# A two-layer transformer on one core: another order for the tail, and two sums moved from GpSimd to VectorE

## The chip, the cores and the metric

The kernel runs on one core of one Trainium2 chip. The core has five engines that work in parallel and wait for each other by semaphores: TensorE (PE in the profile; PEld are its weight loads), VectorE (DVE), ScalarE (ACT), GpSimd (POOL) and SyncE (SP), which here only issues transfers. Each engine takes its instructions strictly in the order of its own list. The metric is the device time of one execution in microseconds, and lower is better. All data is float32.

## The reference

Two transformer layers over 8 batches of 256 tokens with 128 channels. In each layer the normalised and modulated input goes through causal attention, and then through a mixture of experts of which every token uses two. Cut to what matters here, the second layer's expert part is:

```
def _L1_ffn_ref(x, gate_w, gate_b, shared_wg, shared_wu, shared_wd, experts_wg, experts_wu, experts_wd):
    router_logits = sigmoid(x @ gate_w + gate_b)
    expert_values, expert_indices = top_k(router_logits, k=2)
    expert_values = expert_values / sum(expert_values)
    hg = einsum('bsd,edi->bsei', x, experts_wg)          # 16 experts, 64 hidden channels
    hu = einsum('bsd,edi->bsei', x, experts_wu)
    all_outputs = einsum('bsei,eid->bsed', silu(hg) * hu, experts_wd)
    selected = take_along_axis(all_outputs, expert_indices[..., None], axis=2)
    expert_weighted = sum(expert_values[..., None] * selected, axis=2)
    return x + _mlp(x, shared_wg, shared_wu, shared_wd) + expert_weighted

x = x + ga * _L1_attn_ref(layernorm(x) * (1 + ca) + sa, ...)
h = layernorm(x) * (1 + cb) + sb
x = x + gb * _L1_ffn_ref(h, ...)
```

`ga`, `ca`, `sa` and `gb`, `cb`, `sb` are rows of a modulation, one for each batch.

## The kernel before

The 2048 tokens are kept in four wide tiles `x[0]` to `x[3]`, 512 tokens (two batches) each, as 128 partitions by four groups of 128 channels. `TT` is 4, the groups of a wide tile, and `LAST` is 3, the last wide tile. From line 1058 on nothing is reordered by a scheduler: the order of the calls is, engine by engine, the order of the instructions. The loops over layer 0 and over the attention of layer 1 come first. The tail, lines 2016 to 2126, is a list of calls written out by hand; it begins when the last attention scores are done.

In the tail the second layer's experts are computed in two ways.

For the first three wide tiles the tokens have been sorted by expert into a table `xs` in HBM. It is read in 40 small tiles of 128 rows, four at a time, as ten "quads" m = 0 to 9:

- `fetch_rows1(m)` (line 1738) has SyncE load four small tiles. `turn1(m)` (1775) transposes them on TensorE, copies the result to `xT` on ScalarE, and then calls `fetch_rows1(m + 4)`.
- `fetch_weights1(m)` (1753) is for the quads 4 to 9, whose experts are known only at run time: SyncE reads four row numbers and issues four loads of 128 KB into `wt`.
- `hidden1(m)` (1785): eight pairs of matmuls into a PSUM buffer of tag "s" (there are two), Silu on ScalarE, product on VectorE into `aq`.
- `project_tiles(m)` (1798): four matmuls, two copies on VectorE into `ysb` (three buffers), and SyncE stores the 256 KB to the table `ys` in HBM.
- When all of `ys` is written, `gather1(j)` (1900), for j = 0 to 11, has GpSimd issue two indirect transfers each, which bring every token's two expert results into `yg`.
- `combine1(j)` (1906): ScalarE multiplies one result with its weight into `tc` (two buffers), VectorE adds the other times its weight. After each fourth, `tc` is multiplied with the modulation `gb`, added to `x[w]`, and SyncE stores `x[w]` to the output. These two steps are done by GpSimd for w = 0 and 1, and by VectorE for w = 2.

For the last wide tile the experts are computed densely, with eight pairs p = 0 to 7 of experts:

- `dense_hidden(p)` (1849): four matmuls of 512 columns into a buffer of tag "s", Silu on ScalarE, product on VectorE into `a` (the function `gated`, 1842).
- `gate_rows(k)` (1823) transposes the gates of one batch, and SyncE spreads them through HBM over the partitions into `gp`, which `dense_gate(p)` (1855) multiplies with `a` on VectorE.
- `dense_project(p)` (1859): eight matmuls that add to `outs[LAST]` in PSUM.

The shared expert runs over two wide tiles at once: `shared_hidden(w)` (1867) and `shared_project(w)` (1878) for w = 0 and 2. `ffn1_add(w)` (1891) multiplies a wide tile of `outs` with `gb` on VectorE and adds it to `x[w]`.

Between them lie the ends of attention and routing of the last two batches: `spread_last` (1642) and `finish1` (1654) end the attention of batch 7. `norms[0]` and `norms[1]` are lists of five steps for batches 6 and 7 (`norm1`, 1675: measure, normalise with a square root on ScalarE, modulate into `h`, and two steps of GpSimd that make `ht` and add it to `x`). `go6` and `go7` are the steps of `route1` (1699) for these batches, one for each call: logits on TensorE and Exp on ScalarE; first half of the top-2 search on VectorE; second half; weights and gates. `judge` and `flag` (1920) check on VectorE that all softmax sums were in range; the last instruction of the tail writes `bad`, which every engine then loads before a branch around a slower path that is not taken.

ScalarE holds one set of functions at a time: a change between Silu, Exp and square root brings an instruction ACT_TABLE_LOAD.

Of the kernel before, what the change touches and what calls it, by code (L numbers as in the profile page):

```python
# [17 lines left out]
B, S = 8, 256  # L18
# [539 lines left out]
def fast_path(ctx: ExitStack, tc: tile.TileContext, i: dict, out: bass.AP, bad: bass.AP):  # L558
# [224 lines left out]
    def of_batches(rows, w):  # L783

        return rows[:, bass.ts(w, 2), :].unsqueeze(2).to_broadcast([P, 2, 2, P])

    def by_batch(t):
        return t.rearrange("p (b j) c -> p b j c", j=2)
# [807 lines left out]
    def values1(b, u):  # L1596
        v = st1["v", b, u // 2]
        if u == 0:
            st1["s", b] = pp.tile([P, S], F32, tag="sum", bufs=1, name=f"sum1_{b}")
            st1["ou", b] = lp.tile([P, 2, 4, S], F32, tag="ou", name=f"ou1_{b}")  # L1600
        s = st1["s", b]
        o = pp.tile([P, 2, S], F32, tag="o", bufs=1, name=f"o1_{b}_{u}")
        pts = [st1.pop(("pt", b, 2 * u + m)) for m in range(2)]
        for m in range(2):
            for kb, cols, qs in blocks:
                for n in range(2):
                    nc.tensor.matmul(  # L1607
                        out=o[bass.ts(n, D1), m, qs], lhsT=v[:, kb, bass.ts(4 * (u % 2) + 2 * m + n, D1)],
                        rhs=pts[m][:, n, cols], start=(kb == 0), stop=(kb == 1), skip_group_check=True,
                    )  # L1610

        for kb, cols, qs in blocks:
            for m in range(2):
                for n in range(2):
                    nc.tensor.matmul(
                        out=s[bass.ts(2 * n + m, 32), qs], lhsT=on[:, u, :], rhs=pts[m][:, n, cols],
                        start=(kb == 0 and u == 0), stop=(kb == 1 and u == 3), skip_group_check=True,
                    )
        nc.vector.tensor_copy(st1["ou", b][:, :, u, :], o)

    def reciprocals1(b):
        r = st1["r", b] = lp.tile([P, S], F32, tag="r", name=f"r1_{b}")
        nc.vector.reciprocal(r, st1.pop(("s", b)))
        if b == B - 1:
            return

        rd = dp1.tile([2, NC1, S], F32, tag="rd", name=f"rd1_{b}")
        nc.sync.dma_start(out=rd.rearrange("n c q -> (n c) q"), in_=r[0:P:8, :])
        rb = lp.tile([P, 2, 4, S], F32, tag="rb", bufs=1, name=f"rb1_{b}")
        for n in range(2):  # L1630
            nc.sync.dma_start(
                out=rb[bass.ts(n, D1)].rearrange("p m u q -> p (m u q)"),
                in_=rd[n].rearrange("c q -> (c q)").partition_broadcast(D1),
            )
        st1["rb", b] = rb
        judge(r)
# [116 lines left out]
    def fetch_weights1(m):  # L1753

        tag, n = {4: ("wt", 2), 5: ("wt", 2), 9: ("rb", 1)}.get(m, ("v", 3))
        wt = sq["w", m] = lp.tile([P, 4, WD1], F32, tag=tag, bufs=n, name=f"wt1_{m}")
        for t in range(4):
            d = 4 * m + t - E1
            if t == 0:
                _, rs = nc.values_load_multi_w_load_instructions(  # L1760
                    z1.widx[0:1, d : d + 4], engines=[mybir.EngineType.SP], min_val=0, max_val=(E1 - 1) * P,
                    skip_runtime_bounds_check_because="an expert's number, 128 times",
                )
            nc.sync.dma_start(out=wt[:, t, :], in_=i["wpk1"][bass.ds(rs[t], P), :])
# [10 lines left out]
    def turn1(m):  # L1775
        xT_ps = ps_ln([P, 4, P], f"xT1_{m}")
        xg = sq.pop(("x", m))
        for t in range(4):
            nc.tensor.transpose(xT_ps[:, t, :], xg[:, t, :], ident)
        xT = sq["xT", m] = lp.tile([P, 4, P], F32, tag="xT", name=f"xTs1_{m}")  # L1780
        nc.scalar.copy(xT, xT_ps)
        if m + 4 < NQ:
            fetch_rows1(m + 4)

    def hidden1(m):
        xT = sq.pop(("xT", m))
        gu = pp.tile([P, 2, 2, P], F32, tag="s", name=f"gu1_{m}")
        for what in range(2):
            for t in range(4):
                nc.tensor.matmul(  # L1790
                    out=gu[bass.ts(t % 2, I1), what, t // 2, :], lhsT=weights1(m, t)[what],
                    rhs=xT[:, t, :], start=True, stop=True,
                )
        a = sq["a", m] = lp.tile([P, 2, P], F32, tag="aq", name=f"aq1_{m}")
        nc.scalar.activation(a, gu[:, 0], AF.Silu)
        nc.vector.tensor_tensor(a, a, gu[:, 1], ALU.mult)

    def project_tiles(m):
        a = sq.pop(("a", m))
        y = [pp.tile([P, 2, P], F32, tag=tag, bufs=1, name=f"yq1_{m}_{tag}") for tag in ("o", "sum")]  # L1800
        for t in range(4):
            k = t % 2
            nc.tensor.matmul(
                out=y[k][:, t // 2, :], lhsT=a[bass.ts(k, I1), t // 2, :], rhs=weights1(m, t)[2],
                start=True, stop=True,
            )
        ysb = lp.tile([P, 2, 2, P], F32, tag="ysb", bufs=3, name=f"ysb1_{m}")
        for k in range(2):
            nc.vector.tensor_copy(ysb[:, :, k, :], y[k])
        nc.sync.dma_start(  # L1810
            out=z1.ys[bass.ds(4 * m * P, 4 * P), :].rearrange("(t p) c -> p t c", p=P),
            in_=ysb.rearrange("p a k c -> p (a k) c"),
        )
# [92 lines left out]
    def combine1(j):  # L1906
        w, n = divmod(j, TT)
        if n == 0:
            sums[w] = lp.tile([P, TT, P], F32, tag="ht", name=f"tc1_{w}")
        t = sums[w]  # L1910
        yg, g = sums["yg", j // 3][:, j % 3], g12_1[:, j, :]
        nc.scalar.activation(t[:, n, :], yg[:, 0, :], AF.Copy, scale=g[:, 0:1])  # L1912
        nc.vector.scalar_tensor_tensor(t[:, n, :], yg[:, 1, :], g[:, 1:2], t[:, n, :], ALU.mult, ALU.add)  # L1913
        if n == TT - 1:
            eng = nc.gpsimd if w < 2 else nc.vector
            eng.tensor_tensor(by_batch(t), by_batch(t), of_batches(mdb1[:, GB], w), ALU.mult)  # L1916
            eng.tensor_tensor(x[w], x[w], t, ALU.add)  # L1917
            nc.sync.dma_start(out=out[:, bass.ts(w, TT), :], in_=x[w])

    def flag():  # L1920
# [95 lines left out]
    norms = [norm1((b, 1)) for b in (B - 2, B - 1)]  # L2016
    go6, go7 = (one(route1((b, 1))) for b in (B - 2, B - 1))
    values1(*divmod(N - 1, 4))
    reciprocals1(B - 1)
    turn1(0)  # L2020
    hidden1(0)
    turn1(1)
    turn1(2)
    hidden1(1)
    add()
    project_tiles(0)
    fetch_weights1(7)
    turn1(3)
    project_tiles(1)
    fetch_weights1(8)  # L2030
    fetch_weights1(9)
    hidden1(2)
    turn1(4)
    tables()
    hidden1(3)
    norms[0][0]()
    project_tiles(2)
    turn1(5)
    norms[0][1]()
    hidden1(4)  # L2040
    project_tiles(3)
    turn1(6)
    hidden1(5)
    norms[0][2]()
    project_tiles(4)
    turn1(7)
    hidden1(6)
    hidden1(7)
    norms[0][3]()
    project_tiles(5)  # L2050
    go6()
    turn1(8)
    norms[0][4]()
    project_tiles(6)
    turn1(9)
    go6()
    hidden1(8)
    project_tiles(7)
    hidden1(9)
    go6()  # L2060
    project_tiles(8)
    spread_last()
    project_tiles(9)
    for j in range(TT * LAST): gather1(j)
    shared_hidden(0)
    go6()
    finish1(B - 1)
    norms[1][0]()
    gate_rows(0)
    norms[1][1]()  # L2070
    norms[1][2]()
    norms[1][3]()
    shared_project(0)
    go7()
    shared_hidden(2)
    go7()
    dense_hidden(0)
    go7()
    dense_hidden(1)
    go7()  # L2080
    shared_project(2)
    ffn1_add(0)
    dense_hidden(2)
    dense_hidden(3)
    gate_rows(1)
    ffn1_add(1)
    ffn1_add(2)
    dense_hidden(4)
    dense_hidden(5)
    judge(st1["r", B - 1])  # L2090
    norms[1][4]()
    judged = flag()
    next(judged)
    dense_hidden(6)
    dense_gate(0)
    dense_gate(1)
    dense_hidden(7)
    combine1(0)
    dense_gate(2)
    dense_project(0)  # L2100
    combine1(1)
    dense_project(1)
    dense_gate(3)
    dense_project(2)
    dense_project(3)
    combine1(2)
    combine1(3)
    dense_gate(4)
    combine1(4)
    dense_gate(5)  # L2110
    dense_gate(6)
    dense_project(4)
    combine1(5)
    combine1(6)
    combine1(7)
    dense_gate(7)
    dense_project(5)
    combine1(8)
    combine1(9)
    dense_project(6)  # L2120
    dense_project(7)
    combine1(10)
    combine1(11)
    ffn1_add(LAST)
    next(judged, None)
    nc.sync.dma_start(out=out[:, bass.ts(LAST, TT), :], in_=x[LAST])
    manual.close()
    l1.close()

# [93 lines left out]
```

## Time and profile before

| | us |
| --- | --- |
| median of six runs | 642.28 |
| lowest and highest of them | 638.04, 644.18 |
| the profiled execution, measured as a run | 643.22 |
| its span, first to last instruction | 641.4 |

Busy time over the whole span: TensorE 544.3 us (85%), VectorE 347.4 (54%), GpSimd 300.7 (47%), ScalarE 274.3 (43%). The chain that ended last, followed back from the last instruction, is short and lies in the tail. These are its pieces from 619.32 us on, with the start, the length and what ran:

```profile
619.32 0.62 DVE tc L1913 x2
619.94 0.07 issue
620.01 1.66 POOL tc L1916
621.67 0.07 issue
621.74 1.81 POOL x L1917
623.54 0.02 issue
623.56 0.70 ACT tc L1912 x2
...
625.47 3.15 DVE tc L1913 x4
628.62 0.02 issue
628.64 0.70 DVE tc L1916
629.34 0.02 issue
629.37 0.69 DVE x L1917
630.06 0.61 DVE tf L1894
630.67 0.02 issue
630.69 0.69 DVE x L1895
631.38 0.12 DVE bad L1927
```

A row of a timeline, as shown further on, reads: start in us from the span's first instruction, duration, engine (SPq are SyncE's issues), line, operation, what it writes `<-` what it reads, shape, how many in a row; in brackets the engine's idle time before it and what ended that. "Remote" there means that no instruction was found beside the semaphore's change, and "issue" that the profile shows nothing the engine waited for. Ends of matmuls are modelled, their starts are recorded.

### The profile page before, as it was taken

To read this page: it belongs to the slowest core of one execution; us is meant where nothing else is said; L and a number is where in the kernel's file an instruction comes from. 1 tells how busy PE (TensorE), PEld (TensorE's weight loads), DVE (VectorE), ACT (ScalarE), POOL (GpSimd) and SP (SyncE) were. 2 spreads that over 40 slices of the span, in tenths; PEclk is the share of its full clock that TensorE was granted. 3 is DMA by queue.
4 is the path that set the end of the run, shared out by engine and by line. 5 is a ranking of instruction groups with operands and counts; after the bars stand their busy time and mean duration, and the time that the engine had idled before them with its cause. 6 is when DMAs were issued, how large, how long until landed. Compare 5 with 4: busy or idle time off the path is not lost. (4 is left out here: it accounts for less than half of the span.)

```text
span 641.4 us, 11930 instructions
## 1 busy us (share of the span) xinstructions
PE 544.3 (85%) x4391; PEld 384.1 (60%) x4391; DVE 347.4 (54%) x1069; ACT 274.3 (43%) x486; POOL 300.7 (47%) x456
## 2 busy tenths in 40 slices
PE   3798879788699999699999999999999988883580
PEld 3444434455699897566676767666777666650250
DVE  3348897865532221356436664666565766541393
ACT  1485666544155554166334532445353424321130
POOL 7356697866124441465611447513646441047421
PEclk9999988879799999799999999999999998797796
DMA  8999970120349994220302031303030356524031
GB/s 280 344 408 401 388 279 14 55 98 26 108 141 328 308 317 152 108 74 26 88 5 67 9 80 34 80 1 67 21 81 18 72 160 182 166 72 106 20 84 55
DMA packets 52911, 85.41 MB, mean 133 GB/s; under 512 B 6428, under 2 KB 32156, under 8 KB 51692
## 3 DMA queue, kind: packets, MB, share of 16 engines
q1 hardware_dynamic: 44444, 59.77, 29.2%
q0 software_dynamic: 8400, 24.78, 12.2%
q8 instruction: 37, 0.61, 0.4%
q14 instruction: 30, 0.25, 0.1%
HBM read 53.46 MB, written 31.07 MB: 132 GB/s over the span
## 5 line engine op out<-in xcount | busy, mean ns | idle before, releaser
L812 POOL TENSOR_SCALAR_AFFINE_SELECT pt<-pt 128x256 f32<-128x256 f32 (+1 forms) x176 | 88.7, 530 | 108.3 <-ACT pt L1588 79.4
L1047 POOL DMA_INDIRECT yg<-ys,yidx x56 | 53.5, 956 | 52.2 <-DMA ys<-ysb 33.9
L1588 ACT ACTIVATE pt<-sc 128x768 f32<-128x768 f32 x64 | 48.4, 808 | 26.4 <-PE sc L1585 26.3
L1039 POOL DMA_INDIRECT wt<-in_wpk_dram,widx x31 | 29.2, 942 | 51.7 <-PE xT L1329 49.2
L1141 ACT ACTIVATE pt<-sc 128x1024 f32<-128x1024 f32 x48 | 46.5, 1023 | 15.6 <-PE sc L1137 12.4
L1340 ACT ACTIVATE hst<-hp,wt 128x128 f32<-128x128 f32 x136 | 38.9, 368 | 31.5 <-ACT hst L1340 18.8
L1585 PEld LDWEIGHTS sc<-q,k 64*128 64x128 f32 x512 | 41.5, 187 | 16.5 <-issue 11.5
L1585 PE MATMUL sc<-q,k 64*128 64x256 f32 (+1 forms) x512 | 50.5, 336 | 0.0
L1607 PE MATMUL o<-pt,v 128*64 128x256 f32 (+1 forms) x512 | 48.7, 332 | 1.8 <-POOL pt L812 1.8
L1570 ACT COPY v<-vp 128x512 f32<-128x512 f32 x32 | 18.8, 586 | 67.7 <-PE vp L1567 59.6
L1350 DVE COPY ysb<-yt 128x128 f32<-128x128 f32 x39 | 11.4, 292 | 60.4 <-PE yt L1346 60.4
L1607 PEld LDWEIGHTS o<-pt,v 128*64 128x64 f32 x512 | 31.9, 136 | 19.7 <-POOL pt L812 5.6
L1558 DVE COPY q<-qp 128x512 f32<-128x512 f32 x32 | 22.0, 689 | 39.3 <-PE qp L1554 37.7
L1137 PE MATMUL sc<-qm,k 32*128 32x512 f32 x192 | 36.9, 701 | 4.6 <-ACT pt L1141 3.8
L1338 PE MATMUL hp<-xTs,wt 128*128 128x128 f32 x272 | 36.5, 277 | 4.3 <-DMA wt<-in_wpk_dram,widx 3.3
L1554 PE MATMUL qp<-h,wq 128*128 128x256 f32 x128 | 37.1, 413 | 1.3 <-DVE sh L1299 1.3
L924 POOL DMA_INDIRECT xs<-ht0b,idx x32 | 31.7, 990 | 13.5 <-issue 4.6
L1567 PE MATMUL vp<-wv,h 128*128 128x512 f32 x64 | 35.9, 643 | 1.2 <-DVE q L1558 1.2
L1338 PEld LDWEIGHTS hp<-xTs,wt 128*128 128x128 f32 x272 | 33.0, 192 | 5.9 <-issue 2.5
L1346 PE MATMUL yt<-wt,hst 128*128 128x128 f32 x272 | 35.8, 275 | 0.0
L1558 ACT COPY k<-kp 128x512 f32<-128x512 f32 x32 | 18.8, 588 | 35.6 <-PE kp L1554 34.6
L1554 PE MATMUL kp<-h,wk 128*128 128x256 f32 x128 | 33.6, 386 | 0.0
(296 smaller groups left out, 1131.8 us busy)
## 6 DMA issues: line engine op xcount, KB each, us to landing
xs<-zero SPq DMA_DIRECT2D x1, 12288.0 KB
xs<-zero SPq DMA_DIRECT2D x1, 8192.0 KB
rb<-rd SPq DMA_DIRECT2D x14, 512.0 KB
mdb<-mrd SPq DMA_DIRECT2D x2, 2048.0 KB
xg<-xs SPq DMA_DIRECT2D x63, 64.0 KB
wt<-in_wpk_dram SPq DMA_DIRECT2D x24, 128.0 KB
wst<-in_wpk_dram SPq DMA_DIRECT2D x5, 514.0 KB
ys<-ysb SPq DMA_DIRECT2D x10, 256.0 KB
```

The lines of the kernel that those rows point to most:

```text
L812: nc.gpsimd.affine_select(out=pt, in_=pt, compare_op=ALU.is_ge, fill=0.0, base=0, pattern=[[0, pt.shape[1]], [1, P]], channel_multiplier=-1,)
L1047: nc.gpsimd.indirect_dma_start(out=yg[:, k, :], out_offset=None, in_=self.ys[:, :], in_offset=bass.IndirectOffsetOnAxis(ap=self.yidx[:, j, ...
L1137: nc.tensor.matmul(out=sc[:, n, :].rearrange("p (a q) -> p a q", q=rhs.shape[2]), lhsT=k[r, cols], rhs=rhs, start=True, stop=True,)
L1141: nc.scalar.activation(pt[:, bass.ts(half, 2), :], sc, AF.Exp)
L1338: nc.tensor.matmul(out=hp[:, c, :], lhsT=wt[:, bass.ts(c, P)], rhs=xT, start=True, stop=True)
L1340: nc.scalar.activation(hs[:, c, :], hp[:, c, :], AF.Gelu_apprx_tanh, bias=wt[:, WB + c : WB + c + 1])
L1554: nc.tensor.matmul(out=ps_[:, n, :], lhsT=w1[f"w{what}1"][:, bass.ts(2 * u + n, P)], rhs=hb, start=True, stop=True)
L1558: copy(st1[what, b, u], ps_)
L1567: nc.tensor.matmul(out=vp, lhsT=hb[:, bass.ts(j, P)], rhs=w1["wv1"][:, bass.ts(half, 512)], start=True, stop=True)
L1585: nc.tensor.matmul(out=sc[:, n, cols], lhsT=k[r, m, bass.ts(kb, P)], rhs=q[r, m, qs], start=True, stop=True)
L1588: nc.scalar.activation(pt, sc[:, :, 0:384], AF.Exp, scale=1.0 / math.sqrt(D1))
L1607: nc.tensor.matmul(out=o[bass.ts(n, D1), m, qs], lhsT=v[:, kb, bass.ts(4 * (u % 2) + 2 * m + n, D1)], rhs=pts[m][:, n, cols], start=(kb == ...
```

## The change

Two things. In `combine1` the multiplication with `gb` and the sum into `x[w]` are on VectorE for all three wide tiles; GpSimd has none of them any more. And the calls of the tail stand in another order. No call is added or left out, and none changes what it computes.

```
         if n == TT - 1:
-            eng = nc.gpsimd if w < 2 else nc.vector
-            eng.tensor_tensor(by_batch(t), by_batch(t), of_batches(mdb1[:, GB], w), ALU.mult)
-            eng.tensor_tensor(x[w], x[w], t, ALU.add)
+            nc.vector.tensor_tensor(by_batch(t), by_batch(t), of_batches(mdb1[:, GB], w), ALU.mult)
+            nc.vector.tensor_tensor(x[w], x[w], t, ALU.add)
             nc.sync.dma_start(out=out[:, bass.ts(w, TT), :], in_=x[w])
```

The order of the calls, before and after, stage by stage (several calls to a line; `g6` is `go6()`, `n0.2` is `norms[0][2]()`, `hid`, `proj`, `turn` are `hidden1`, `project_tiles`, `turn1`):

```
before:
 turn0 hid0 turn1 turn2 hid1 add proj0 fetch_weights1(7) turn3 proj1 fetch_weights1(8) fetch_weights1(9)
 hid2 turn4 tables hid3 n0.0 proj2 turn5 n0.1 hid4 proj3 turn6 hid5 n0.2 proj4 turn7 hid6 hid7 n0.3
 proj5 g6 turn8 n0.4 proj6 turn9 g6 hid8 proj7 hid9 g6 proj8 spread_last proj9
 gather1 x12  shared_hidden(0) g6 finish1(7) n1.0 gate_rows(0) n1.1 n1.2 n1.3
 shared_project(0) g7 shared_hidden(2) g7 dense_hidden(0) g7 dense_hidden(1) g7 shared_project(2)
 ffn1_add(0) dense_hidden(2) dense_hidden(3) gate_rows(1) ffn1_add(1) ffn1_add(2)
 dense_hidden(4) dense_hidden(5) judge n1.4 flag (minimum) dense_hidden(6) dense_gate(0) dense_gate(1)
 dense_hidden(7) combine1(0) dense_gate(2) dense_project(0) combine1(1) dense_project(1) dense_gate(3)
 dense_project(2) dense_project(3) combine1(2) combine1(3) dense_gate(4) combine1(4) dense_gate(5)
 dense_gate(6) dense_project(4) combine1(5..7) dense_gate(7) dense_project(5) combine1(8) combine1(9)
 dense_project(6) dense_project(7) combine1(10) combine1(11) ffn1_add(3) flag (bad) store x[3]
after:
 turn0 turn1 hid0 hid1 turn2 add proj0 fetch_weights1(7) turn3 proj1 fetch_weights1(8)
 hid2 turn4 tables hid3 n0.0 proj2 hid4 turn5 n0.1 turn6 proj3 n0.2 proj4 hid5 g6 turn7
 proj5 hid6 hid7 fetch_weights1(9) n0.3 g6 n0.4 turn8 proj6 hid8 turn9 proj7 g6 hid9 proj8 spread_last proj9
 finish1(7) g6 n1.0  gather1 x12  shared_hidden(0) gate_rows(0) n1.1 n1.2 shared_hidden(2) n1.3
 g7 g7 shared_project(0) shared_project(2) g7 dense_hidden(0) ffn1_add(0) dense_hidden(1) g7
 dense_hidden(2) n1.4 ffn1_add(1) dense_hidden(3) gate_rows(1) dense_hidden(4) dense_hidden(5) ffn1_add(2)
 judge dense_gate(0) dense_gate(1) dense_hidden(6) dense_hidden(7) dense_project(0) dense_gate(2)
 dense_gate(3) dense_project(1) dense_project(2) combine1(0) dense_project(3) combine1(1) combine1(2)
 dense_gate(4) combine1(3) dense_gate(5) combine1(4) dense_gate(6) dense_gate(7) combine1(5..7)
 flag (minimum) dense_project(4) combine1(8) dense_project(5) dense_project(6) combine1(9) combine1(10)
 dense_project(7) combine1(11) ffn1_add(3) store x[3] flag (bad)
```

## The prediction

> **What bounds the kernel now.** I read the times first, then the chain that ended last, then each engine's timeline from 515 us on. Before 525.7 us the two programs hold the same instructions; from there to the end the order differs. Four stages follow one another in this tail.
>
> *Stage 1, 526 to 568 us: SyncE's queue.* The timeline of SyncE's issues (start, us, what) and two of VectorE's rows:
>
> ```profile
> 541.90 4.69 SPq L1764 DMA_DIRECT2D wt<-in_wpk_dram  x8
> 546.84 1.88 SPq L1035 DMA_DIRECT2D xg<-xs  x4
> 548.82 0.38 SPq L1810 DMA_DIRECT2D ys<-ysb  x1
> 549.45 1.92 SPq L1035 DMA_DIRECT2D xg<-xs  x4
> 551.47 14.21 SPq L1810 DMA_DIRECT2D ys<-ysb  x7
> ```
>
> ```profile
> 551.30 0.42 DVE L1809 COPY ysb<-yq_o 128x256 f32<-128x256 f32 x1 [2.14 <-DMA ys<-ysb]
> 553.95 0.43 DVE L1809 COPY ysb<-yq_o 128x256 f32<-128x256 f32 x1 [1.79 <-DMA ys<-ysb]
> ```
>
> SyncE issues one transfer about every half microsecond without a pause: eight weight loads (quads 8 and 9), then the rows of quad 8, a result store, the rows of quad 9, and so on. The stores are late, so VectorE waits 2.14 and 1.79 us for a free `ysb` buffer, and TensorE stands behind it. The stage ends when the tenth store lands.
>
> *Stage 2, 568 to 601 us: the gathers.*
>
> ```profile
> 568.55 1.01 POOL L1047 DMA_INDIRECT yg<-ys,yidx  x1 [22.39 <-DMA ys<-ysb]
> 569.86 0.96 POOL L1047 DMA_INDIRECT yg<-ys,yidx  x1 [0.31 <-issue]
> ...
> 597.41 0.95 POOL L1047 DMA_INDIRECT yg<-ys,yidx  x1 [0.30 <-issue]
> 598.38 0.73 POOL L1683 TENSOR_TENSOR ht<-xn1b,mdb 128x256 f32<-128x256 f32 x1
> ```
>
> ```profile
> 590.02 0.60 ACT L1846 ACTIVATE a_('s', 2)_5980<-gus 128x512 f32<-128x512 f32 x1 [8.86 <-remote]
> 600.54 0.60 ACT L1846 ACTIVATE a<-gud 128x512 f32<-128x512 f32 x1 [9.93 <-remote]
> ```
>
> GpSimd waits for the stores, then issues 24 gathers 1.25 us apart. Meanwhile ScalarE starts `a_('s', 2)` at 590.02 and the first dense `a` at 600.54, though TensorE's rows for both inputs end at 578.6 and 580.5. So TensorE's results become known 11 and 20 us late. The logits `lg`, VectorE's wait at 579.40, were 4 us late. These three announcements, lg, gus(2) (of `shared_hidden(2)`) and gud (of `dense_hidden(0)`), are 10.6 and 10.5 us apart. By the next hand-over, at 602.71, the gathers are over. I do not know the cause and treat the lateness as tied to the gathers.
>
> *Stages 3 and 4, 601 to 631.5 us: VectorE.* Windows (length; busy time and instructions of PE, PEld, DVE, ACT, POOL; clock, DMA share, GB/s):
>
> ```profile
> 568.00:601.00 33.00, 14.98 (x76) 7.59 (x74) 6.30 (x25) 4.47 (x7) 25.18 (x28) 0.76 0.35 80
> 601.00:617.00 16.00, 13.46 (x30) 5.65 (x31) 12.91 (x30) 4.60 (x10) 0.52 (x1) 0.86 0.28 67
> 617.00:632.00 15.00, 8.32 (x65) 7.21 (x63) 14.40 (x25) 3.34 (x12) 6.36 (x4) 0.92 0.14 54
> ```
>
> VectorE works 6.30 of 33 us during the gathers and 12.91 + 14.40 = 27.31 of the 31 us after them. So the end is set by VectorE's backlog, and GpSimd lengthens it:
>
> ```profile
> 620.01 1.65 POOL L1916 TENSOR_TENSOR tc<-tc,mdb 128x512 f32<-128x512 f32 x1 [18.49 <-DVE tc L1913]
> 621.74 1.80 POOL L1917 TENSOR_TENSOR x<-x,tc 128x512 f32<-128x512 f32 x1
> ```
>
> ```profile
> 620.45 1.35 DVE L1913 SCALAR_TENSOR_TENSOR tc<-yg,g,tc 128x128 f32<-128x128 f32 x1
> 621.73 2.35 DVE L1857 TENSOR_TENSOR a<-a,gp 128x512 f32<-128x512 f32 x2
> ```
>
> A `tc` update takes 0.34 us alone and 1.35 beside GpSimd's multiply. The last `x` add ends at 631.38; the flag, its loads and the branch fill the rest of the 641.4 us and are the same in both programs.
>
> **The change, part by part.**
>
> *The weights of quad 9 go behind the store of quad 5.* From the first load of quad 8 (541.90) to the first rows of quad 8 (546.84) are 4.94 us for two quads, so one quad costs 2.47. Removing it brings the rows of quad 8 to 544.4, store 2 from 548.82 to 546.35, store 3 from 551.47 to 549.0. A row load issued at 548.36 let TensorE go on at 549.88, 1.5 us later, and store 2 freed `ysb` at 551.28, 2.46 after its issue. So `ysb` of quad 5 is copied at 548.8, not 551.30; store 5 leaves at 550.0. The displaced weights issue from 550.5 to 553.0 and land at 554.6. That wait is new: store 6 stands behind them (ready 552.5, issued 553.05, and nobody needs it before 557), and `hidden1(9)` starts at 554.6 instead of 557.43, a gain of 2.8. From there on the order also moves the second half of a top-2 search (559.48 to 560.48, 1.0 us) ahead of the wait for the weights, where VectorE is idle; of this I count 0.4, since the copies also wait for TensorE. Stage 1 ends 3.2 us earlier: the tenth store goes from 565.33 to 562.1, the first gather from 568.55 to 565.3. Bounds: 0, if the weights land 3 us late, and 4.0, if all of the 1.0 counts.
>
> *`finish1`, `go6` and `norms[1][0]` ahead of the gathers.* GpSimd's queue is unmoved by it: its listing has the same 24 gathers, the same four normalisation steps before and after. On TensorE the 32 matmuls of `y` (3.84 us) now precede `shared_hidden(0)` (1.9), but VectorE has five gate steps (0.9) in between, and the statistics are followed by ScalarE's square root after a Silu (0.6). `h` of the last batch is ready 5.8 us after the first gather; it was 5.5. I count 0. SyncE's list after the tenth store is the same in both programs, the store of `x[3]` included, which is only written ahead of the flag.
>
> *`shared_hidden(2)` ahead of `go7`.* One more table load on ScalarE: 1.28 us by the row at 579.88. It lies in an idle stretch of 8.86 us. Without that cover it costs 1.28. [...]
>
> *The waits of stage 2.* TensorE's results are now announced in the order gus(2), lg, first gud; before it was lg, gus(2), gud. They are as many, so I keep the 32.0 us from the first gather (568.55) to the first dense `a` (600.54), which then comes at 597.3. The bounds are one announcement, 10.5 us, to either side (rivals 1 and 3).
>
> *The sums of tiles 0 and 1 on VectorE.* Four more instructions; the same form for tile 2 runs 628.64, 629.37, 629.98: 0.73 and 0.61 from start to start, so 1.34 a tile, 2.7 in all. Gone are GpSimd's four (1.65, 1.80, 1.65, 1.26) and what they do to VectorE: 1.01 in the `tc` at 620.45, 1.07 in the second `a` at 622.33, 1.01 and 1.08 in the `tc` at 625.39 and 626.67, together 4.2. ScalarE's 4.50 us wait for GpSimd's `x` ends too; the buffer of `tc` is now freed by VectorE well before it is needed. Net -1.5.
>
> *The order of the dense stage on VectorE.* The second top-2 half of batch 7 (1.1 us) falls into stage 2's idle time: -1.1. But the adds that filled VectorE's waits move. Now, waiting for the third `a` (ScalarE done at 606.33), VectorE did `ffn1_add(0)`; the new order has done that already, so it idles 1.4. Before the fifth `a` (611.66) it did two adds, 2.6 us; one of them is now left after the sixth, so it idles 2.3. Before the sixth, 1.1. Together 4.8 where the rows show 0.47, 1.02 and 0.85, or 2.3: +2.5. The flag's minimum (0.42) is only moved. Bounds 0 to +4: 0 if TensorE runs ahead, 4 if each hand-over stays late.
>
> Twice a `tc` multiply now directly follows the update it reads, 0.37 us after its start instead of 0.26 (628.27 to 628.64): +0.2.
>
> Sum: -3.2 + 0 + 0 - 1.5 - 1.1 + 2.5 + 0.2 = **-3.1 us**. Of the profiled execution (643.22, 1.82 around its span of 641.4) that leaves 640.1. That execution lies 0.94 above the median of the six runs, 642.28; from the median it is **639.2 us**.
>
> **The rivals.**
>
> 1. *The late announcements shrink.* The page cannot say what holds them back; TensorE's rows are over by 580.5 us, and the stage has a new order. One of them saved is 10.5 us more: 628.7. For it: nowhere else in the trace is a result known so late. Against it: GpSimd's burst is as long and as dense as before.
>
> 2. *The transfer was hidden anyway.* The displaced weights land 3 us late, or the gathers' stage takes up what stage 1 gives: 642.3. For it: SyncE's queue is full until 553 us, and the load now needs the very time it frees. Against: both `ysb` waits and TensorE's waits for rows hang on that queue.
>
> 3. *Slower: one more late announcement.* Place: TensorE, between the shared and the dense stage. The first dense gud now stands behind the projection of `a_('s', 2)`, which waits for gus(2) to be known; before, it was issued at once. If three announcements become four before VectorE's first dense `a`, it costs 10.5 us: 642.3 - 3.1 + 10.5 = 649.7. It decides as soon as lg and gus(2), neighbours on TensorE, are held back one after the other and both count. For it: the measured 10.6 and 10.5 us are per result, not per stage. Against: the announcement at 602.71 came 2.2 us after the one before, once the gathers were over.
>
> **How the numbers follow.** Forecast 0.48, with its own range 636 to 642.5 (stage 1 from 0 to -4.0, the dense stage's order from 0 to +4); rival 1 0.17; rival 2 0.14; rival 3 0.21. A measurement of this kernel tells about 0.5%, 3.2 us, from no change: faster is below 639.1, slower above 645.5. The forecast's middle lies at that edge, so half of it (0.24) is faster and half is the same. Faster: 0.24 + 0.17 = 0.41; same: 0.24 + 0.14 = 0.38; slower 0.21. To leave no more than 0.2 outside, the range reaches into rivals 1 and 3: 630 to 649.
>
> **What would show it.** First gather near 565.3 us and no `ysb` wait on a store above 1 us: stage 1 right. VectorE's `tc` updates all near 0.34 us: GpSimd no longer slows it. VectorE idle about 1.4, 2.3 and 1.1 us before the third, fifth and sixth dense `a`: the order's price. First dense `a` 32 us after the first gather: the lateness is the gathers'; 22 or 42 us would be rivals 1 and 3. A first gather at 568 us or later would refute the largest term.

## The result, and the profile after

The changed kernel takes 643.87 us (median of 36 runs), the kernel before 643.54 us (78 runs beside them). The ratio is 1.0005, with a 95% interval of 0.9991 to 1.0018: no change, where 3.1 us less was forecast. The profiled execution has a span of 641.8 us; before it was 641.4.

*Stage 1.* SyncE's issues in the changed kernel (start, us, what):

```profile
544.08 1.89 SPq L1035 DMA_DIRECT2D xg<-xs  x4
546.07 0.38 SPq L1810 DMA_DIRECT2D ys<-ysb  x1
546.69 1.91 SPq L1035 DMA_DIRECT2D xg<-xs  x4
548.70 1.53 SPq L1810 DMA_DIRECT2D ys<-ysb  x3
551.38 2.42 SPq L1764 DMA_DIRECT2D wt<-in_wpk_dram  x4
553.90 9.16 SPq L1810 DMA_DIRECT2D ys<-ysb  x4
```

The rows of quad 8 leave at 544.08 where it was 546.84, and the loads of quad 9 (551.38) stand behind the store of quad 5. Two rows of VectorE, then `hidden1(9)` on TensorE, in the changed kernel and in the kernel before:

```profile
543.02 0.42 DVE L1809 COPY ysb<-yq_o 128x256 f32<-128x256 f32 x1 [1.46 <-DMA ys<-ysb]
548.64 0.42 DVE L1809 COPY ysb<-yq_o 128x256 f32<-128x256 f32 x1 [3.41 <-DMA ys<-ysb]
```

```profile
554.96 1.80 PE L1790 MATMUL gu<-xTs,wt 128*64 128x128 f32 x16 [0.70 <-DMA wt<-in_wpk_dram]
```

```profile
557.43 1.24 PE L1790 MATMUL gu<-xTs,wt 128*64 128x128 f32 x16
```

The waits for a free `ysb`, which were to be no longer than 1 us, are 1.46 and 3.41 us (2.14 and 1.79 before), though the copy for quad 5 itself comes at 548.64, as forecast (548.8): in the new order VectorE reaches these copies sooner and waits longer. `hidden1(9)` now waits for its weights. The chain that ended last says the same, and shows what comes before and after:

```profile
550.27 0.92 SPq L1760
551.38 3.45 DMA wt<-in_wpk_dram
554.96 1.80 PE gu L1790 x16
...
579.01 20.92 another core or an unknown queue
```

The loads of quad 9, and SyncE's reading of their four row numbers (line 1760) ahead of them, lie on the chain that sets the end; and 20.92 us of it are time for which no releaser is found.

*Stage 2.* GpSimd's first and last gather, and ScalarE's last two Silu groups of the stage:

```profile
565.88 1.01 POOL L1047 DMA_INDIRECT yg<-ys,yidx  x1 [22.46 <-DMA ys<-ysb]
...
594.72 0.95 POOL L1047 DMA_INDIRECT yg<-ys,yidx  x1 [0.30 <-issue]
```

```profile
575.58 0.60 ACT L1846 ACTIVATE a_('s', 2)_5961<-gus 128x512 f32<-128x512 f32 x1 [4.49 <-issue]
...
599.96 1.08 ACT L1846 ACTIVATE a<-gud 128x512 f32<-128x512 f32 x2 [20.94 <-remote]
```

The first gather starts 2.67 us earlier (565.88, was 568.55), but the first dense `a` only 0.58 (599.96, was 600.54). Of the three late announcements one is left: gus(2) and lg are known at once, and then the first two gud together, 16 us after the second's last row. From first gather to first dense `a` it is 34.08 us instead of 31.99.

*Stages 3 and 4.* VectorE's products of the dense `a` that wait, and windows over the tail (columns as in the prediction):

```profile
605.78 0.69 DVE L1847 TENSOR_TENSOR a<-a,gud 128x512 f32<-128x512 f32 x1 [1.63 <-ACT a L1846]
...
608.70 0.69 DVE L1847 TENSOR_TENSOR a<-a,gud 128x512 f32<-128x512 f32 x1 [0.90 <-ACT a L1846]
...
612.09 0.69 DVE L1847 TENSOR_TENSOR a<-a,gud 128x512 f32<-128x512 f32 x1 [2.38 <-ACT a L1846]
613.81 0.69 DVE L1847 TENSOR_TENSOR a<-a,gud 128x512 f32<-128x512 f32 x1 [1.03 <-ACT a L1846]
```

```profile
600.00:617.00 17.00, 14.05 (x26) 5.58 (x26) 10.20 (x21) 4.42 (x8) 0.00 (x0) 0.78 0.25 59
617.00:632.00 15.00, 8.34 (x66) 7.53 (x66) 14.66 (x32) 3.82 (x13) 0.00 (x0) 0.98 0.16 57
```

GpSimd has nothing to do after 600 us, and no `tc` update is above 0.35 us. VectorE waits 1.63, 0.90, 2.38 and 1.03 us for dense `a`. From the first dense `a` to the end of the last `x` add it takes 31.90 us; before it was 30.84.

The sum: the tail's first instruction that both programs share (the copy of turn 0 on ScalarE, 526.42 before, 525.70 after) came 0.72 us earlier, ahead of any change. From there: first gather -1.96, first dense `a` +2.09, last `x` add +1.06, the rest -0.04. That is +1.15, less 0.72 gives the +0.43 between the two spans (641.40 and 641.84).

One thing must be known for all that follows. The kernel before took 642.3 to 643.8 us (medians) here (this chip's number is not on record) and, twice, on the chip numbered 7, and 624.3 to 625.9 us on the four other chips that the experiments ran on; no median lies between. Most of the difference is the late announcements: on those four chips there are none. In the kernel before the first dense `a` comes 31.99 us after the first gather here and 13.57 us on chip 15. Ratios are always to runs of the kernel before that were made beside the experiment on the same chip; "with lateness" and "without" say which chip it was. Times of single profiles are given from the start of turn 0's copy.

### The profile page after: what moved, and what is told of

It is laid out like the page before. It is cut to its first block, busy times and chain, and to the rows that moved or that the text cites. A ratio compares the mean times of both kernels' runs of the same rounds, so it can differ in the third digit from the quotient of the medians.

```text
span 641.8 us, 11933 instructions
## 1 busy us (share of the span) xinstructions
PE 550.7 (86%) x4391; PEld 390.2 (61%) x4391; DVE 343.0 (53%) x1073; ACT 275.4 (43%) x487; POOL 294.1 (46%) x452
## 4 chain that ended last, share of the span: by engine, by line
PE 62%; DVE 16%; DMA 8%; ACT 4%; issue 4%; another core or an unknown queue 3%; POOL 1%; SPq 1%; DVEq 0%; POOLq 0%; ACTq 0%
PE sc L1585 7%; PE o L1607 6%; PE qp L1554 5%; PE vp L1567 5%; PE kp L1554 4%; PE hp L1338 4%; PE y L1660 4%; PE yt L1346 4%; DMA wt<-in_wpk_dram,widx 4%; PE sc L1137 3%; PE sum L1615 3%; PE o L1162 2%; PE hp L1272 2%; PE qk L1101 1%
## 5 line engine op out<-in xcount | busy, mean ns | idle before, releaser
L1340 ACT ACTIVATE hst<-hp,wt 128x128 f32<-128x128 f32 x136 | 38.9, 368 | 29.9 <-ACT hst L1340 20.0
L1585 PEld LDWEIGHTS sc<-q,k 64*128 64x128 f32 x512 | 41.5, 187 | 16.5 <-issue 11.5
L1558 DVE COPY q<-qp 128x512 f32<-128x512 f32 x32 | 22.0, 689 | 40.6 <-PE qp L1554 40.6
L1350 DVE COPY ysb<-yt 128x128 f32<-128x128 f32 x39 | 11.4, 292 | 59.1 <-PE yt L1346 59.1
```

The costliest lines, as they stand in the source:

```text
L1558: copy(st1[what, b, u], ps_)
L1585: nc.tensor.matmul(out=sc[:, n, cols], lhsT=k[r, m, bass.ts(kb, P)], rhs=q[r, m, qs], start=True, stop=True)
```

## The experiments

**1. The two parts with a place of their own, each alone** (without lateness). The sums on VectorE are the diff of `combine1` shown above, in the old order. The weights alone:

```
     fetch_weights1(8)
-    fetch_weights1(9)
     hidden1(2)
...
     project_tiles(5)
+    fetch_weights1(9)
     go6()
```

> The kernel before with one part of the change: the sums of tiles 0 and 1 into x are done by VectorE. Theory (the prediction's term): VectorE takes 2.7 us of work and is spared 4.2 us of GpSimd's slowdown, so the last x add ends 1.5 us earlier, the tc updates all take about 0.34 us, and the time falls by 0.2 per cent (ratio 0.998). Rival: the slowdown lay beside waits for TensorE, the spared 4.2 us reappear as idle time of VectorE, and the time does not fall (ratio 1.000 to 1.002).

> The kernel before with one part of the change: the weight loads of quad 9 stand on SyncE's queue behind the store of quad 5. Theory A: the first gather comes 2 to 3 us earlier (565.5 to 566.5 where it was 568.55), and everything behind it moves with it: first dense a near 598, ratio 0.995 to 0.997. Theory B: the gain is given back at the late announcements: first gather 565.5 to 566.5 too, but the first dense a stays at 599.5 to 601 us, ratio 1.000.

Sums alone: 0.9992 (0.9966 to 1.0018). Weights alone: 1.0015 (0.9990 to 1.0041). Neither can be told from no change by its time. The profiles tell more: from the first dense `a` to the end of the last `x` add it is 32.48 us with the sums on VectorE and 33.67 to 33.72 in three profiles with GpSimd's (both kernels before of experiments 2 and 3, and this one with the weights alone). So the sums are worth 1.2 us; 1.5 was forecast. With the weights alone `hidden1(9)` starts at 30.14 and waits for them, and the first gather comes at 41.97: nothing is gained, where both theories had it 2 to 3 us earlier.

**2. The row of gathers broken by memsets** (without lateness). `gather1` calls the function that it is given, here `nc.gpsimd.memset(most, P - 0.5)`, behind each of its gathers:

```
-    for j in range(TT * LAST): gather1(j)
+    for j in range(TT * LAST):
+        gather1(j, apart_on_gpsimd)
```

> The changed kernel with a 128x1 memset on GpSimd behind each of the 24 gathers, which keeps them from following one another without another instruction between. Theory A (TensorE's results are announced late because the gathers follow one another without a break): the first dense a comes within 3 us of the end of TensorE's rows for it, near 583 us instead of 599.96, and the kernel ends 8 to 17 us earlier (ratio 0.974 to 0.988). Theory B (the lateness is tied to the stretch of time in which the gathers' transfers run, or to something on TensorE): first dense a at 599 to 601 us, ratio 1.000. By either, the gathers stay about 1.26 us apart.

> The kernel before with the same memset behind each gather. Theory A: lg, gus(2) and gud are known within 1 us of TensorE's rows (575 to 583 us instead of 579.4, 590.0 and 600.5); the end comes 8 to 17 us earlier (ratio 0.974 to 0.988). Theory B: the three announcements stay 10.5 us apart, ratio 1.000.

0.9978 (0.9962 to 0.9995) in the changed kernel and 1.0010 (0.9988 to 1.0032) in the kernel before. The first dense `a` came at 578.76 and 579.42 us. That looked like theory A, but the kernel before took 625.94 us beside it without any memset, and the kernels of experiment 1, on the same chip, had no lateness either: the test said nothing.

**3. Both kernels again, and the two parts together** (without lateness).

> The kernel before, unchanged, profiled on the chip of this call. In the last call's four profiles no result of TensorE was late (first dense a at 578 to 580 us) and the kernel before took 625.9 us, not 643.5. Theory A (the lateness belongs to the chip or the moment, not to the program): either lg, gus(2) and gud are late here and the time is near 643 us, or none is and the time is near 626 us; nothing between. Theory B (the memset or a part of the change took it away): the kernel before shows late results here and the time is 640 us or more, also where the other runs of this call show none.

> The changed kernel, unchanged, in the same call. If results are late: first dense a near 600 us as before, ratio 0.999 to 1.002. If none is late: the first gather comes 2 to 3 us earlier than in the kernel before and the end follows by only a part, ratio 0.996 to 0.999, because by then VectorE's work after the last gathers sets the end.

> The kernel before with the two parts that have a place of their own, the weight loads of quad 9 behind the store of quad 5 and the sums of tiles 0 and 1 on VectorE, in the old order of everything else. Theory A (the rest of the reordering is worth nothing or costs): ratio at or below that of the changed kernel. Theory B (the rest of the reordering is what gains): ratio 0.999 to 1.002, above that of the changed kernel by 0.002.

The copy of the kernel before came out at 0.9986 (0.9969 to 1.0002) of itself, which is how finely such a comparison can tell; the changed kernel at 0.9986 (0.9964 to 1.0009), the two parts in the old order at 0.9975 (0.9952 to 0.9998). So without lateness, too, the change is worth about 1 us (2.3 at most, by the interval), and no gain of the reordering beyond its two parts is seen. ScalarE's rows of the kernel before on this chip:

```profile
576.82 0.60 ACT L1846 ACTIVATE a_('s', 2)_5980<-gus 128x512 f32<-128x512 f32 x1 [1.87 <-PE gus L1872]
579.38 0.60 ACT L1846 ACTIVATE a<-gud 128x512 f32<-128x512 f32 x1 [1.96 <-PE gud L1852]
```

`a_('s', 2)` starts at 576.82 and the first dense `a` at 579.38, released by TensorE's own rows. In the same program on the first chip these were 590.02 and 600.54.

**4. The displaced load moved further up** (without lateness). In the changed kernel:

```
     norms[0][2]()
+    fetch_weights1(9)
     project_tiles(4)
...
     hidden1(7)
-    fetch_weights1(9)
     norms[0][3]()
```

> The changed kernel with the weight loads of quad 9 one store earlier still on SyncE's queue, behind the store of quad 3 instead of quad 5. In the changed kernel's profiles hidden1(9) starts when these loads land (wait on wt, 0.7 and 1.7 us). Theory A (the displaced load is what comes last in stage 1): hidden1(9) starts 1 to 1.7 us earlier, 27 to 28 us after the start of turn 0's copy instead of 29.2, and the first gather comes as much earlier, 38.5 to 39.5 us after that copy instead of 40.1; the kernel's ratio is 0.001 to 0.003 below the changed kernel's. Theory B (the half clock of TensorE or the stores behind it come last): the first gather stays at 40 to 41 us after the copy.

0.9939 (0.9909 to 0.9969). `hidden1(9)` on TensorE, and GpSimd's first gather, in this kernel (turn 0's copy at 523.81 us):

```profile
551.51 1.09 PE L1790 MATMUL gu<-xTs,wt 128*64 128x128 f32 x16
```

```profile
562.26 1.00 POOL L1047 DMA_INDIRECT yg<-ys,yidx  x1 [20.74 <-DMA ys<-ysb]
```

The matmuls no longer wait, start at 27.70 and take 1.09 us; the first gather comes at 38.45. Theory A holds: the displaced load is what came last in stage 1. The time gained against the changed kernel's ratio of experiment 3 (on another chip) is 0.005, more than the 0.001 to 0.003 that it gave.

**5. VectorE's waits filled with sums** (without lateness). Three orders of the dense stage of the changed kernel, in which `tc` has three buffers of another tag and the store of `x[0]` follows `ffn1_add(0)`. The calls of `ffn1_add`, `dense_gate`, `judge` and `flag` move too, so what is gained is not the sums' alone. The first puts `combine1(0)` to `combine1(3)` ahead of `dense_hidden(0)` and `gate_rows(1)` behind it; the second (and the third, with memsets between the gathers) is:

```
     dense_hidden(0)
     dense_hidden(1)
+    gate_rows(1)
+    combine1(0)
+    combine1(1)
+    combine1(2)
+    combine1(3, store=False)
     dense_hidden(2)
...
     dense_hidden(3)
+    combine1(4)
+    combine1(5)
...
     dense_hidden(5)
+    combine1(6)
+    combine1(7)
...
```

> The changed kernel with the sums of the first eight gathered column tiles moved up into VectorE's idle time between the dense a, the first four ahead of the first dense a, and the gate rows of the second half right behind the first. Theory (VectorE's backlog after the gathers sets the end): 5.3 us of work (eight tc updates of 0.34 and two sums of 1.3) leave the tail; without late results VectorE idles only 5.9 us after 575 us, of which most is filled: 4 to 6 us less than the changed kernel (ratio 0.988 to 0.993); with late results only the first four and one sum are early: 2 to 3 us less. Rival (TensorE or the landing of the last gather sets the end): under 1 us.

> The changed kernel with the sums of the first eight gathered column tiles in VectorE's waits of the dense stage, now behind the second dense a, and the gate rows of the second half right behind that a too, so that TensorE isn't held by their buffer. Without late results: VectorE's idle time from 575 us on falls from 5.9 us to under 2 us, the last x add ends 9 to 11 us after the last gather has landed instead of 14.2, ratio 0.990 to 0.994. With late results (first dense a at 600 us): little is moved out of the tail, ratio 0.996 to 1.002. Rival (TensorE's clock sets the end): ratio 0.997, as the kernel with the sums ahead of the first dense a had it.

> The same kernel with a 128x1 memset on GpSimd behind each gather. If results are late in this call's other profiles: by theory A (the unbroken row of gathers holds them back) not in this one, first dense a near 580 us and 15 us or more below the others; by theory B (not the row) as late as in the others. If none is late: the same time as without the memsets, ratio within 0.002 of it.

The first: 0.9969 (0.9947 to 0.9991), a miss. The transposes of `gate_rows(1)`, between the first two dense groups, had TensorE wait 1.81 us for the gates and then 2.65 us for a PSUM buffer of tag "s"; VectorE stood 3.86 us. The second: 0.9934 (0.9912 to 0.9957); the third 0.9924 (0.9893 to 0.9955). Windows over the dense stage, first of the changed kernel of experiment 3, then of the second order:

```profile
575.00:592.00 17.00, 15.19 (x45) 6.29 (x41) 12.32 (x33) 6.01 (x10) 13.02 (x14) 1.00 0.47 108
592.00:609.50 17.50, 8.63 (x66) 7.60 (x66) 16.62 (x32) 3.87 (x13) 5.36 (x6) 0.92 0.28 78
```

```profile
577.00:594.00 17.00, 15.98 (x65) 7.64 (x66) 15.04 (x42) 9.36 (x19) 13.04 (x14) 1.00 0.68 148
594.00:610.00 16.00, 10.32 (x69) 9.08 (x67) 15.60 (x26) 2.06 (x5) 7.13 (x8) 0.89 0.21 69
```

In the first 17 us VectorE (third pair of figures) is busy 15.04 instead of 12.32. The last `x` add ends 10.5 us after the last gather has landed; in the changed kernel it was 14.2.

**6. Again with lateness: both edits together, and the memsets.** These ran on chip 7, where the kernel before took 643.83 us.

> The changed kernel with both edits that gained: the weight loads of quad 9 behind the store of quad 3, and the sums of eight gathered column tiles in VectorE's waits. Theory (the two act on different stages and add up): first gather 38.5 to 39.5 us after turn 0's copy, VectorE without idle time over 1 us from then on, ratio 0.985 to 0.990. Rival (VectorE's whole work from 575 us on is the bound, and an earlier start of the gathers does not start it earlier): ratio 0.992 to 0.995, as either edit alone.

> The changed kernel, unchanged. Without late results: ratio 0.996 to 1.000, first gather 40 to 41 us after turn 0's copy, first dense a 53.5 to 54.5 us after it. With late results: first dense a 34 us after the first gather, ratio 0.999 to 1.002.

> The changed kernel with a 128x1 memset on GpSimd behind each gather. With late results in after_third: theory A (the unbroken row of gathers) first dense a within 15 us of the first gather and 12 to 18 us less time; theory B as late as there. Without: the time of after_third within 0.003.

The changed kernel: 1.0009 (0.9981 to 1.0037). With memsets: 1.0005 (0.9980 to 1.0029). Both edits together: 0.9974 (0.9954 to 0.9994), above what either theory gave (0.985 to 0.990, 0.992 to 0.995). It is the only one of the three that is faster than the kernel before on a chip with lateness, and 0.0035 below the changed kernel beside it. It was not run on a chip without, where each half gave 0.992 to 0.994. ScalarE and TensorE of the kernel with memsets:

```profile
601.86 1.08 ACT L1848 ACTIVATE a<-gud 128x512 f32<-128x512 f32 x2 [22.85 <-remote]
```

```profile
581.24 0.59 PE L1854 MATMUL gud<-h,wg 128*128 128x512 f32 x1 [0.83 <-issue]
582.67 0.59 PE L1854 MATMUL gud<-h,wg 128*128 128x512 f32 x1 [0.84 <-issue]
584.77 0.64 PE L1854 MATMUL gud<-h,wu 128*128 128x512 f32 x1 [1.51 <-issue]
586.18 1.01 PE L1854 MATMUL gud<-h,wu 128*128 128x512 f32 x1 [0.77 <-issue]
```

The first dense `a` starts 34.10 us after the first gather; in the other two kernels it is 34.04 and 34.11. So the break between the gathers changes nothing: theory A of experiment 2 falls. The rows of TensorE show something new. The four matmuls of the second gud, 0.59 to 1.01 us each, have 0.77 to 1.51 us of "issue" ahead of them, time in which nothing shown holds them: in this profile it is not only the announcement that is late, the matmuls themselves come out slowly. The other two profiles of this experiment don't show it.

**7. Half of the gathers, and the gathers at the end.** The first edit leaves out half of the gathers; the later sums take the rows of earlier ones, so its result is not the reference's.

```
-    for j in range(TT * LAST): gather1(j)
+    for j in range(TT * LAST // 2): gather1(j)
...
-        yg, g = sums["yg", j // 3][:, j % 3], g12_1[:, j, :]
+        yg, g = sums["yg", j // 3 % 2][:, j % 3], g12_1[:, j, :]
```

> The changed kernel with only the first 12 of the 24 gathers; the sums of column tiles 6 to 11 take the gathered rows of tiles 0 to 5 instead of their own. Theory G (results are held back as long as the row of gathers runs): where the kernel before takes 640 us or more, the first dense a comes 18 to 20 us after the first gather instead of 34, and the time falls by about 14 us. Theory P (the lateness belongs to the place in the program or to TensorE alone): first dense a 33 to 35 us after the first gather, time within 3 us. Where the kernel before takes 626 us: first dense a 13.5 us after the first gather by both, and 0 to 4 us less time.

> The changed kernel with all 24 gathers behind the last dense a on GpSimd (a 128x1 product of that a ahead of them makes GpSimd wait for it). Theory G: no dense a is late on any chip, the first comes 53 to 56 us after turn 0's copy and the eighth 13 to 17 us later; the gathers then end near 100 us after that copy, and the kernel takes 630 to 640 us on any chip. Theory P: where the kernel before takes 640 us or more the first dense a comes 70 us or more after the copy, and the kernel takes over 655 us.

Both fell on a chip without lateness. Half of the gathers: 0.9922 (0.9881 to 0.9962). All gathers behind the last dense `a`: 1.0326 (1.0189 to 1.0464) from two runs; the first gather came at 72.35, and then every column tile waited some 2 us for its own, up to 102.8. That is slower than theory G's 630 to 640 us, and says nothing about lateness. Half of the gathers was run twice more.

> The changed kernel with only the first 12 of the 24 gathers; the sums of column tiles 6 to 11 take the gathered rows of tiles 0 to 5. Theory G (results are held back as long as the row of gathers runs): where the kernel before takes 640 us or more, the first dense a comes 18 to 20 us after the first gather instead of 34, and the kernel takes 12 to 16 us less than before. Theory P (the place in the program): 33 to 35 us after the first gather, time within 4 us of before. Where the kernel before takes 626 us: as in the last call, 13 us after the first gather and 0.992 of the time.

> The changed kernel with only the first 12 of the 24 gathers; the sums of column tiles 6 to 11 take the gathered rows of tiles 0 to 5. Theory G (results are held back as long as the row of gathers runs): where the kernel before takes 640 us or more, the first dense a comes 18 to 20 us after the first gather instead of 34, and the kernel takes 12 to 16 us less than before. Theory P (the place in the program): 33 to 35 us after the first gather, time within 4 us of before. Where the kernel before takes 626 us: 13 us after the first gather and 0.993 of the time, as it did twice.

Once without lateness, 0.9930 (0.9918 to 0.9943), and once on chip 7: 0.9731 (0.9645 to 0.9818), 626.09 us beside 643.48. GpSimd and ScalarE of that last profile:

```profile
569.49 1.01 POOL L1047 DMA_INDIRECT yg<-ys,yidx  x1 [23.65 <-DMA ys<-ysb]
...
583.33 0.95 POOL L1047 DMA_INDIRECT yg<-ys,yidx  x1 [0.30 <-issue]
```

```profile
586.68 1.09 ACT L1846 ACTIVATE a<-gud 128x512 f32<-128x512 f32 x2 [4.54 <-remote]
```

The first dense `a` starts 17.19 us after the first gather instead of 34, and 2.4 us after GpSimd has issued the last one (584.28). 17.4 us are gained; without lateness the same edit gave 4.0 and 4.9. So some 13 us are lateness that went with the second half of the row. That rules out theory P (33 to 35 us) and is close to theory G's 18 to 20: how late the first dense `a` is goes with the length of the row. It rests on one profile and two runs. That every result is held back as long as the row runs was not seen: in the kernel before lg and gus(2) became known at 579.40 and 590.02, within the row, and in the changed kernel gus(2) and lg at once. What in the row does it, the transfers or GpSimd's instructions, was not tried apart, and no kernel with its gathers at the end ran on chip 7.

## Why the prediction was wrong

**Stage 1, -3.2 us: the step that failed.** Its first half was right: the rows of quad 8 leave SyncE 8.6 us after its first store instead of 11.4, so one quad of loads is worth 2.9 (2.47 was taken). Its second half was not. I let the displaced loads issue from 550.5 to 553.0 and land at 554.6, where before `hidden1(9)` started at 557.43, a gain of 2.8. They issued from 551.38 to 553.80, in an execution that was 0.72 ahead, since 1.15 us pass on SyncE between the store of quad 5 and the first load. 0.92 of them are the reading of the four row numbers, which takes 0.31 at most in the kernel before. `hidden1(9)` started on them at 554.96. That is rival 2, which got 0.14: the load now needs the time that it freed. In this pair of profiles 1.96 us were left of 3.2. One pair is not the size of it, though. From turn 0's copy, over all profiles with the gathers in their place:

| | start of `hidden1(9)` | first gather | profiles |
| --- | --- | --- | --- |
| order and loads of the kernel before | 30.5 (29.6 to 31.0) | 41.5 (40.6 to 42.1) | 4 |
| stage 1 of the changed kernel | 29.4 (28.8 to 29.8) | 41.2 (40.1 to 43.3) | 11 |
| order of the kernel before, loads behind the store of quad 5 | 29.0 (27.9, 30.1) | 41.2 (40.4, 42.0) | 2 |
| loads behind the store of quad 3 | 27.4 (27.1, 27.7) | 38.9 (38.5, 39.3) | 2 |

`hidden1(9)` gains 1.1 us and not 2.8, and waits for the weights in all eleven. And in six of the eleven the way from there to the first gather is 12.1 to 13.9 us; in the other five, as in the kernel before, it is 10.9 to 11.1, so that at the gathers 0.3 us of the mean are left.

The granted clock tells the six from the five. TensorE is busy almost all of this way. In the six a stretch of 3.4 or 6.8 us at half clock begins from 0.24 us before to 0.72 us after the start of `hidden1(9)`, and the mean clock to the first gather is 0.76 to 0.87; in the five it is 1.00. One profile of each, both of the changed kernel as it is (experiments 6 and 3): the row of `hidden1(9)`, and the window from there to the first gather, with the clock 0.86 and 1.00 (columns as in the prediction):

```profile
556.67 2.48 PE L1790 MATMUL gu<-xTs,wt 128*64 128x128 f32 x16 [1.72 <-DMA wt<-in_wpk_dram]
556.67:568.90 12.23, 12.23 (x82) 10.00 (x84) 4.81 (x10) 0.38 (x1) 0.00 (x0) 0.86 0.32 89
```

```profile
552.79 1.80 PE L1790 MATMUL gu<-xTs,wt 128*64 128x128 f32 x16 [1.69 <-DMA wt<-in_wpk_dram]
552.79:563.68 10.89, 10.89 (x82) 8.86 (x84) 4.71 (x10) 0.38 (x1) 0.00 (x0) 1.00 0.34 99
```

In the four profiles of the kernel before, no such stretch begins on this way. So the late load seems to cost twice: the wait itself, and in six of eleven profiles a slower TensorE behind it; that the wait brings the half clock on is not shown. Experiment 4 is the test: with the load two stores earlier the wait is gone (0.34 us of it in the second of the two profiles), and 2.6 us arrive. In that second one the way to the first gather is 12.3 us at full clock, so the clock is not all that lengthens it.

**Stage 2, "I keep the 32.0 us": wrong by 2.1.** The lateness was there and was tied to the gathers, as I took it; but it is not a price per result. In all four profiles of the new order with the whole row and lateness the first dense `a` comes 34.04 to 34.11 us after the first gather, with one late announcement as with several before. The hand-over at 602.71, which the prediction took as prompt, was late as well: TensorE's rows for it had ended at 595.17, and it was known at 602.68. Rivals 1 and 3, 10.5 us to either side for an announcement more or less, rested on that reading and had no ground. That 32.0 became 34.1 rests on a single profile of the kernel before with lateness; why is open.

**The sums on VectorE, -1.5 us: right,** 1.2 in the profiles without lateness (experiment 1). No `tc` update of the tail is above 0.35 us in the changed kernel's first profile, as forecast, where it was up to 1.42.

**The order of the dense stage and the `tc` dependency, -1.1 +2.5 +0.2: right in kind.** The waits forecast before the third, fifth and sixth dense `a` were 1.4, 2.3 and 1.1; they are 1.63, 2.38 and 1.03. The 0.90 before the fourth was not forecast. With the sums the stages after the first dense `a` were to take 0.1 us more; in the three profiles with lateness they take 1.06, 0.14 and 0.95 more. Part of it is TensorE, which the prediction left out: after 17.48 us without work the matmuls of two dense groups ran slowly (2.07, 1.92, 1.91 and 1.42 us for two each), before it was one (2.08 and 1.91, then 1.06 and 1.02). The second of them is what the fourth `a` waits for.

**`finish1`, `go6`, `norms[1][0]` and the extra table load at 0: right.** gus(2) and lg are known by 575.6 and 576.8, earlier than before, and the last table load (577.73, 1.28 us) ends 20.9 us before ScalarE's next instruction.

Put together with lateness, three profiles of the changed kernel against the one of the kernel before: -0.5 to -2.0 where -3.2 stood, +2.1 where 0 stood, and +0.1 to +1.1 where +0.1 stood, so from turn 0's copy the last `x` add comes 1.2 to 1.7 us later. The medians differ by 0.3 us only; with one profile on the other side the sum closes no better. Without lateness stage 2 drops out, and what is left is the 0.9986 of experiment 3, about 1 us.

## What to carry to other kernels

When a transfer is moved back in a queue to let others through, it becomes the candidate for the last arrival: work out its own arrival against its own consumer, with every gap on the queue (here 1.15 us ahead of its loads), before the gain of the others is booked; a place between the two may bring most of it, as two stores earlier did here (2.6 us). A wait whose cause is unknown must not be given a unit: the "10.5 us per result" was a property of one trace, and only an experiment on its suspected source (half of the gathers) showed what it goes with. And where one engine sets the end, look for what its idle stretch could already do: in the changed kernel of experiment 3 the gathers of the first eight column tiles were issued by 583.5 us, and their sums were made from 597.25 us on.

## What the runs showed of the hardware that was not expected

- During a row of 24 indirect transfers issued by GpSimd, 1.25 us apart, TensorE's results become known up to 20 us late on chip 7 (and in the first measurement) and at once on four others, with the same program: 643.5 against 624 to 626 us. Halving the row leaves 3.5 us of it (first dense `a` 17.19 us after the first gather, against 13.63 and 13.66); a memset between the transfers changes nothing. The traces differ in one more thing: the six with lateness hold 6796 to 6953 semaphore updates, the fourteen without 8296 to 8525. What differs between the chips was not found.
- In the first profiles of both kernels TensorE's granted clock is 1.00 or 0.50, in stretches of 3.4, 6.8, 10.2, 17.1, 20.5 us and more, each a multiple of 3.413 us except the last, which runs past the end of the span. What sets the clock is not shown. In the six profiles named above half clock came with waits of 1.03 to 1.72 us for the weights. The length of the wait alone does not decide: after 1.69 us in another profile the clock stayed full. The sixteen matmuls of `hidden1(9)` took 2.48 to 3.07 us in the six, 1.80 to 1.91 at full clock behind a wait, and 1.09 at full clock without one.
- Without any change between them, profiles of one program differ by 1.5 us in a stage (first gather at 40.57 and 42.13 in the kernel before, 40.10 and 41.62 in the changed one). A forecast of 3 us from single rows is near what one pair of profiles can show.
